# An adaLN block on one core: a fixed setup order, buffer clears on another queue, and a re-cut passage from attention to the experts

## The chip, the core and the metric

The kernel runs on one core of one Trainium2 chip. A core has five engines that run their own instruction streams in order: TensorE (PE, matrix products, with weight loads shown apart as PEld), VectorE (DVE), ScalarE (ACT), GpSimd (POOL) and SyncE (SP, which here only issues transfers). Engines wait for each other on semaphores. Transfers (DMAs) are issued by SP, ACT or POOL and carried by 16 DMA engines. The metric is the device time of one execution in microseconds (us); less is better.

## The reference, cut to what matters

Two batches of 2048 tokens of width 256 pass through one block: layer norm with a shift and scale made from `c`, attention in a window of 128 tokens (16 heads of 64), a gated sum onto `x`, a second norm, and a mixture of 8 experts with two choices per token and a capacity of 640 tokens per expert and choice.

```python
x = L0_attn_x
mod = (_silu(L0_c) @ L0_wmod).reshape(L0_c.shape[0], 6, 1, -1)
sa, ca, ga, sb, cb, gb = (mod[:, 0], mod[:, 1], mod[:, 2], mod[:, 3], mod[:, 4], mod[:, 5])
ga = (2 * (ga >= 0) - 1) * jnp.maximum(jnp.abs(ga), 0.25)      # gb likewise
h = _layernorm(x, axis=-1) * (1 + ca) + sa
x = x + ga * _L0_attn_ref(h, L0_attn_Wqkv, L0_attn_Wout)
h = _layernorm(x, axis=-1) * (1 + cb) + sb
x = x + gb * _L0_ffn_ref(h, L0_ffn_gate_w, ...)
...
for c in range(K):                       # in _L0_ffn_ref: two choices, 8 experts
    pos = jnp.take_along_axis(jnp.cumsum(oh, axis=0) - 1, idx[:, None], axis=1)[:, 0]
    keep = pos < CAP
    buf_idx = jnp.where(keep, idx * CAP + pos, n_slots)
    xbuf = jnp.zeros((n_slots, Dm), x.dtype).at[buf_idx].set(x, mode='drop')
    hmid = jax.nn.relu(jnp.einsum('ecd,edf->ecf', xb, W1) + b1[:, None, :])
    yb = jnp.einsum('ecf,efd->ecd', hmid, W2) + b2[:, None, :]
    y = y + ytok * (prb * keep.astype(prb.dtype))[:, None]
```

## The kernel before

**Products in three passes.** Operands of the large products are split into a rounded high part and a low remainder: ACT copies the high part (`nc.scalar.copy`), and DVE or POOL subtracts it from the raw value for the low part (`split`, line 124). `passes` (227) then multiplies high by high, high by low and low by high.

**Setup** (322 to 463). SP loads `c`, the first x group, wmod (two loads), six pieces of wqkv and two halves of wout; ACT's queue loads three small tensors. `load_split` (139) loads a piece into a `raw` buffer, of which the pools `stage` and `sp` have two each, and splits it; the low parts of wqkv pieces 1, 2 and 4 and of wout half 1 are made on POOL, the rest on DVE. From `c` come the modulation columns `cols` (PE, DVE) and the rows `wide4` (441 to 453), which go to memory as `rowd` and come back spread over all partitions (`rows`, `gbr`). A tile `blank` (461), which takes a `raw` buffer of `stage` too, holds an empty row. The order of this part is the planner's, which places each instruction by its own estimate of times.

**Attention** runs in a written-out order. From line 1156 on, `tc.manual_schedule` makes every engine, SP among them, follow the program's order. Tokens go in 16 groups of 256; each group has 8 pairs of heads; an iteration `w` (1084) takes two pairs, so there are NW = 64 iterations and three more to drain. It pipelines four stages: new pairs get scores (PE), then masking: `pack` (510) copies the own block on ACT (line 526) and lays the earlier block over it with DVE's masked copy (`copy_predicated`, 527), `maximum` (534) and ACT's `exps`; pairs one iteration older are normalized (POOL); pairs two older are transposed (`turn`), masked on POOL (`unpack`, 584 and 588) and multiplied by the values; pairs three older go through wout (`out_project`), for which a half of wout serves four head pairs of each group, the second half the last four. PE's results lie in a ring of six PSUM banks (`bank`).

**Side work** is put into places of an iteration by hand: `place(work, w, at)` (1039) says at which letter (A, B, M, H, C, S, V, in this order within an iteration) of which iteration the next step of a generator is traced. C stands just before the scores and `pack`, S just after `pack`, V at the end. So are placed the norm of the next group (`NORM`), the eleven steps of `close(g)` (633: gated sum, store, second norm, routing, counting, scatter of the rows to `xbuf` with POOL's indirect transfers; `CLOSE`, and `LATE` for the last groups), the weights of experts 0 and 1 (`Expert.steps`, 177: load, split), and the first item of expert work. At the start of iterations 1 to 4, `clear` (465) fills four pieces of `xbuf` each, 16 in all, from `blank`; ACT's queue issues them.

**Passage and experts.** Each expert's up to 10 tiles of 128 rows are cut into items (840 to 846): expert 0 in five of 2 tiles (q = 0 to 4), expert 1 in 4, 2, 2, 2 (q = 5 to 8), the others from 6 or 4. An item is loaded from `xbuf` (`load_slots`, 859), transposed and split (`turn_slots`, 877), and goes through `first_layer` and `second_layer` for 8 slices of the hidden width (`layers`, 1049). So that items 0 and 1 can begin before the last groups are routed, the last two groups' rows are kept out of the first EARLY = 4 tiles of expert 0: `totals` (737) counts what earlier groups brought and `shift` moves the late rows behind. In `close`, `totals` writes its product into the bank `cnt` ahead of the two products for `counts`, and DVE reads it as `both` (744). After the loop (1162 on) the last steps of `close(15)` alternate with item 1's layers, then item 5 runs, then item 2, the rest of expert 0 under run-time conditions (`further`, 1238), item 6, and so on.

Of the kernel before, what the change touches and what calls it, by code (L numbers as in the profile page):

```python
# [8 lines left out]
FP = mybir.dt.float32  # L9
FR = mybir.dt.float32r  # L10
I32 = mybir.dt.int32
# [17 lines left out]
def adaln_block_kernel(  # L29
# [41 lines left out]
    EARLY = 4 * P  # L71
# [62 lines left out]
    def load(src, shape, name, pool=stage):  # L134
        raw = pool.tile(shape, FP, tag="raw", name=f"raw_{name}", bufs=2)
        nc.sync.dma_start(out=raw, in_=src)
        return raw

    def load_split(hi, lo, src, shape, name, scale=None, pool=stage, eng=nc.vector):
        split(hi, lo, load(src, shape, name, pool), scale, eng)  # L140
# [99 lines left out]
    def norm(g):  # L240
# [13 lines left out]
        for k in range(ND):  # L254
            for t in range(SBT):
                nc.tensor.transpose(
                    tp[:, k * TS + t * P : k * TS + (t + 1) * P], z[:, t, k * P : (k + 1) * P], ident
                )
        hT = wk.tile([P, ND, TS], FP, tag="t2", name=f"hT_{g}")
# [61 lines left out]

    first = norm(0)
    with tc.tile_pool(name="setup", bufs=1) as sp:
# [5 lines left out]
        nc.sync.dma_start(out=wm[:, :, 0 : 2 * D], in_=wmv[:, :, 0 : 2 * D])  # L329
        gw = sp.tile([E, D], FP, name="gw")  # L330
        nc.scalar.dma_start(out=gw, in_=gate_w)
        b1r = sp.tile([E * NF, P], FP, name="b1r")
        nc.scalar.dma_start(out=b1r, in_=b1.rearrange("e (k p) -> (e k) p", p=P))
        nc.scalar.dma_start(
            out=gbias, in_=gate_b.rearrange("(a e) -> a e", a=1).to_broadcast([P, E])
        )
        make_identity(nc, ident)
# [30 lines left out]

        sg = sp.tile([B * ND, P], FP, name="sg")
# [3 lines left out]
        nc.vector.tensor_tensor(sg, sg, cr, ALU.mult)  # L373
        tp = bank("tp_c")
        nc.tensor.transpose(tp[:, 0 : B * ND], sg, ident[0 : B * ND, 0 : B * ND])
        scT = sp.tile([P, B, ND], FP, name="scT")
        nc.vector.tensor_copy(scT.rearrange("p b k -> p (b k)"), tp[:, 0 : B * ND])
        mc = bank("mod_cols")
        for m in range(2):
            for d in range(ND):  # L380
                o = (m * ND + d) * B
                for k in range(ND):
# [6 lines left out]
                    )  # L389
        colf = cols.rearrange("p m d b -> p (m d b)")  # L390
# [4 lines left out]

        for _ in first:
            pass

        for i in range(2):
            for j in range(3):  # L400
                f = slice(j * HD + i * HD // 2, j * HD + (i + 1) * HD // 2)
                load_split(
                    wq[:, 0, :, f], wq[:, 1, :, f], wqkv[:, f].rearrange("(k p) f -> p k f", p=P),
                    [P, ND, HD // 2], f"wq{i}_{j}", QSCALE if j == 0 else None,
                    pool=sp if (3 * i + j) % 2 else stage,
                    eng=nc.gpsimd if j == 1 or (i, j) == (0, 2) else nc.vector,
                )
        nc.sync.dma_start(out=wm[:, :, 2 * D :], in_=wmv[:, :, 2 * D :])
        for i in range(2):
            s = slice(i * NP // 2, (i + 1) * NP // 2)  # L410
            load_split(
                wo[:, 0, s, :], wo[:, 1, s, :],
                wout[i * HD // 2 : (i + 1) * HD // 2, :].rearrange("(k p) d -> p k d", p=P),
                [P, NP // 2, D], f"wo{i}", pool=stage if i else sp,
                eng=nc.gpsimd if i else nc.vector,
            )
        part(*project_qk(0, 0, 0))

# [8 lines left out]
        nc.vector.tensor_copy(b1T, tp[:, 0 : E * NF])  # L427

# [4 lines left out]
        for g in range(2):  # L433
# [16 lines left out]
            if g == 0:  # L450
                nc.vector.tensor_copy(wide4[:, 1, :], plain)
            else:
                nc.vector.tensor_scalar(wide4[:, 2, :], plain, 1.0, None, ALU.add)
        nc.sync.dma_start(out=rowd, in_=wide4)
# [3 lines left out]


        xs[1] = load_x(1)  # L460
        blank = stage.tile([P, ROW], FP, tag="raw", name="blank")
        nc.gpsimd.memset(blank, 0.0)
        nc.gpsimd.memset(blank[:, TOK : TOK + 1].bitcast(I32), 2 * T)

    def clear(i):

        for r0 in range(i * BUF, (i + 1) * BUF, CAP):
            nc.scalar.dma_start(
                out=xbuf[r0 : r0 + CAP, :].rearrange("(p n) d -> p n d", p=P),
                in_=blank.rearrange("p (a d) -> p a d", a=1).to_broadcast([P, CAP // P, ROW]),  # L470
            )

# [160 lines left out]
    def close(g):  # L633
# [103 lines left out]
        def totals(j, o):  # L737

            nc.tensor.matmul(
                out=cnt[:, o : o + KC * E], lhsT=ones,  # L740
                rhs=pref[:, j, :, :].rearrange("p k e -> p (k e)"), start=True, stop=True,
            )
            both = small.tile([P, KC, E], FP, tag="both", name=f"both_{g}_{o}", bufs=2)
            nc.vector.tensor_scalar(
                both.rearrange("p k e -> p (k e)"), cnt[:, o : o + KC * E], float(CAP), None, ALU.min
            )
            total = small.tile([P, E], FP, tag="total", name=f"total_{g}_{o}", bufs=2)
# [3 lines left out]
        if late:  # L751

            e = g - (NG - 2)
            total = totals(j0, n)
            nc.vector.tensor_scalar(
                shift[:, e : e + 1], total[:, e : e + 1], -1.0, float(EARLY), ALU.mult, ALU.add
            )
            nc.vector.tensor_scalar(shift[:, e : e + 1], shift[:, e : e + 1], 0.0, None, ALU.max)
# [7 lines left out]
        nc.vector.tensor_copy(counts, cnt[:, 0:n])  # L766
        yield
# [36 lines left out]
        if late:  # L804
            rows_of = NSLOT - EARLY
# [26 lines left out]
        if g == NG - 1:  # L832

            total = totals(NT, n)
# [8 lines left out]
    for e in range(E):  # L843
        head = 2 if e == 0 else 4 if e in (1, E - 1) else WIDE
        ends = [0, *range(head, NB + 1, 2)]
# [31 lines left out]
    def turn_slots(q, n0):  # L877

        tiles = items[q][1]
        if n0 == 0:  # L880
            w = len(tiles)
            if q and (w > 2 or items[q - 1][0] in (1, E - 1) and items[q - 1][1].start == 0):
                w = WIDE
            xTs[q] = [
# [412 lines left out]
```

## Time and profile before

| What | us |
|---|---|
| median of three runs (lowest, highest) | 1161.58 (1160.19, 1163.09) |
| the profiled execution | 1161.56 |
| its span, first to last instruction | 1159.8 |
| PE busy in the span | 1086.3 (94%) |
| weight loads busy | 999.6 (86%) |
| DVE busy | 877.4 (76%) |
| ACT busy | 676.7 (58%) |
| POOL busy | 593.8 (51%) |
| mean granted clock of PE | 0.970 |

The page gives busy time of each engine, the span in 40 slices with the PE clock that was granted (1.00 is full), groups of instructions by line with their mean duration and the idle time of the engine before them, and the transfers with the time from issue to landing. In a timeline, a line has the start, the duration, the engine (ACTq and SPq are the queues that issue transfers), the line of the kernel, the operation, output and inputs, and in brackets how long the engine stood before it and what released it. L127 is the subtraction or copy in `split`, L232 any product in `passes`.

### The profile page before, as it was taken

To read this page: it belongs to the slowest core of one execution; us is meant where nothing else is said; L and a number is where in the kernel's file an instruction comes from. 1 tells how busy PE (TensorE), PEld (TensorE's weight loads), DVE (VectorE), ACT (ScalarE), POOL (GpSimd) and SP (SyncE) were. 2 spreads that over 40 slices of the span, in tenths; PEclk is the share of its full clock that TensorE was granted. 3 is DMA by queue.
4 is the path that set the end of the run, shared out by engine and by line. 5 is a ranking of instruction groups with operands and counts; after the bars stand their busy time and mean duration, and the time that the engine had idled before them with its cause. 6 is when DMAs were issued, how large, how long until landed. Compare 5 with 4: busy or idle time off the path is not lost. (4 is left out here: it accounts for less than half of the span.)

```text
span 1159.8 us, 25187 instructions
## 1 busy us (share of the span) xinstructions
PE 1086.3 (94%) x9246; PEld 999.6 (86%) x9246; DVE 877.4 (76%) x2168; ACT 676.7 (58%) x2097; POOL 593.8 (51%) x769
## 2 busy tenths in 40 slices
PE   6799999999999999999999997779889999999995
PEld 4678999999999888999999896768879999999995
DVE  6556688888878778888878877767667777878764
ACT  4467776777777567777777676423344444344441
POOL 4235465665675556665675665433522615443524
PEclk9899999999999999999999998879989999999998
DMA  6890010010010010010010022233432524342413
GB/s 228 194 218 21 1 39 19 21 39 19 21 39 19 21 43 29 21 36 20 17 37 20 18 65 70 85 91 95 83 106 87 84 84 90 83 89 67 83 45 36
DMA packets 59571, 72.09 MB, mean 62 GB/s; under 512 B 4807, under 2 KB 51152, under 8 KB 59436
## 3 DMA queue, kind: packets, MB, share of 16 engines
q1 hardware_dynamic: 36988, 44.27, 12.2%
q0 software_dynamic: 11712, 14.79, 7.4%
q10 hardware_dynamic: 10736, 11.27, 4.3%
q8 instruction: 80, 1.31, 0.5%
q14 instruction: 55, 0.45, 0.1%
HBM read 40.11 MB, written 32.27 MB: 62 GB/s over the span
## 5 line engine op out<-in xcount | busy, mean ns | idle before, releaser
L937 ACT ACTIVATE hm<-ph,b1T 128x256 fp32r<-128x256 f32 (+2 forms) x184 | 99.3, 540 | 224.8 <-PE ph L232 192.6
L232 PE MATMUL pq<-hh,wq 128*128 128x256 f32 x1024 | 216.8, 295 | 3.5 <-ACT hh L268 3.0
L232 PE MATMUL ph<-xT,we 128*128 128x256 f32 (+2 forms) x1104 | 203.6, 325 | 15.5 <-DVE xT L127 4.6
L550 ACT ACTIVATE pm<-pm,mx 128x128 f32<-128x128 f32 x512 | 204.1, 402 | 19.4 <-DVE mx L536 16.7
L232 PE MATMUL y<-we,hm 128*128 128x256 f32 x1440 | 201.5, 285 | 6.6 <-DVE hm L939 6.6
L232 PEld LDWEIGHTS y<-we,hm 128*128 128x128 f32 x1440 | 186.7, 190 | 10.7 <-DVE hm L939 9.3
L232 PEld LDWEIGHTS ph<-xT,we 128*128 128x128 f32 x1104 | 172.3, 196 | 21.2 <-issue 6.5
L584 POOL TENSOR_SCALAR_AFFINE_SELECT pT<-pT 128x512 f32<-128x512 f32 (+1 forms) x128 | 80.9, 632 | 211.6 <-ACT pT L583 211.5
L232 PEld LDWEIGHTS pq<-hh,wq 128*128 128x128 f32 x1024 | 170.0, 193 | 5.8 <-ACT hh L268 3.4
L938 DVE TENSOR_SCALAR r<-ph,b1T 128x256 f32<-128x256 f32 (+2 forms) x184 | 101.8, 562 | 73.1 <-ACT hm L937 65.6
L560 POOL TENSOR_TENSOR pm<-pm,rd 128x512 f32<-128x512 f32 x128 | 133.8, 1045 | 28.5 <-DVE rd L558 26.4
L232 PE MATMUL pq<-hl,wq 128*128 128x256 f32 x512 | 145.8, 285 | 0.0
L526 ACT COPY pm<-sc 128x256 f32<-128x256 f32 (+1 forms) x256 | 80.6, 363 | 107.9 <-PE sc L502 70.3
L1002 POOL TENSOR_TENSOR ys<-ys,gw 128x256 f32<-128x256 f32 x56 | 48.4, 971 | 175.7 <-DVE ys L992 157.0
L607 PE MATMUL av<-pT,v 128*64 128x128 f32 (+1 forms) x1472 | 126.7, 321 | 4.7 <-POOL pT L588 2.2
L607 PEld LDWEIGHTS av<-pT,v 128*64 128x64 f32 x1472 | 91.1, 140 | 33.7 <-POOL pT L588 4.6
L1003 POOL DMA_INDIRECT out_dram<-ys,tok x60 | 98.1, 1634 | 33.5 <-issue 11.4
L527 DVE COPY_PREDICATED pm<-within,sc 128x256 f32<-128x256 int32 (+1 forms) x256 | 96.1, 422 | 22.0 <-ACT pm L526 21.1
L502 PE MATMUL sc<-kr,qh 64*128 64x256 f32 (+1 forms) x1024 | 105.7, 296 | 5.0 <-DVE ql L300 2.0
L550 ACT ACTIVATION_READ_ACCUMULATOR pm<-pm,mx 128x1 f32 x512 | 99.6, 194 | 0.0
L232 PEld LDWEIGHTS pq<-hl,wq 128*128 128x128 f32 x512 | 99.0, 193 | 0.0
L939 DVE TENSOR_TENSOR hm<-r,hm 128x256 fp32r<-128x256 f32 (+2 forms) x144 | 94.6, 657 | 5.3
(162 smaller groups left out, 2261.9 us busy)
## 6 DMA issues: line engine op xcount, KB each, us to landing
raw_w<-in_L_ffn_W_dram SPq DMA_DIRECT2D x32, 512.0 KB, 3.9
xbuf<-blank ACTq DMA_DIRECT2D x16, 685.0 KB, 9.6
xt<-xbuf SPq DMA_DIRECT2D x8, 822.0 KB, 4.9
x<-in_L_attn_x_dram SPq DMA_DIRECT2D x16, 256.0 KB, 2.8
out_dram<-x SPq DMA_DIRECT2D x16, 256.0 KB, 2.3
xt<-xbuf SPq DMA_DIRECT2D x7, 548.0 KB, 5.0
raw_wq<-in_L_attn_Wqkv_dram SPq DMA_DIRECT2D x6, 512.0 KB, 7.0
wm<-in_L_wmod_dram SPq DMA_DIRECT2D x1, 1024.0 KB, 11.1
```

What stands on the lines that cost most here:

```text
L232: nc.tensor.matmul(out=out_, lhsT=a, rhs=b, start=start and n == 0 and i == 0, stop=stop and n == last and i == 2, **kw,)
L502: nc.tensor.matmul(out=sc[h][:, t, lo:], lhsT=q[r, t * P : (t + 1) * P], rhs=kr[r, (0, 1, 0)[i], hp, blk, :], start=(i == 0), stop=(i == 2),)
L526: nc.scalar.copy(pm[:, h, ts, :], blocks[:, own, :])
L527: nc.vector.copy_predicated(pm[:, h, ts, :], within.rearrange("p (a k) -> p a k", a=1).to_broadcast([P, n, P]), blocks[:, before, :],)
L550: nc.scalar.activation(pm[:, h, t, :], pm[:, h, t, :], AF.Exp, bias=mx[:, h, t : t + 1], accum_out=den[:, h, t : t + 1],)
L560: nc.gpsimd.tensor_tensor(pmv, pmv, rd.rearrange("p h (t a) -> p (h t) a", a=1).to_broadcast([P, 2 * SBT, P]), ALU.mult,)
L584: nc.gpsimd.affine_select(out=pT[:, :, t0:, 0, :], in_=own[:, :, t0:, :], pattern=[[0, 2], [0, n], [-1, P]], compare_op=ALU.is_gt, fill=0. ...
L607: nc.tensor.matmul(out=av[h * DH : (h + 1) * DH, q0 : q0 + hi - lo], lhsT=v[:, f0 + h * DH : f0 + (h + 1) * DH], rhs=pT[:, h, lo:hi], star ...
L937: nc.scalar.activation(hh[:, s], phv, AF.Relu, bias=bias)
L938: nc.vector.tensor_scalar(r[:, s], phv, bias, 0.0, ALU.add, ALU.max)
L939: nc.vector.tensor_tensor(hl, r[:, 0:W], hh, ALU.subtract)
L1003: add = nc.gpsimd.indirect_dma_start(out=of, out_offset=bass.IndirectOffsetOnAxis(ap=tok[:, 0:1], axis=0), in_=y, in_offset=None, bounds_c ...
```

## The change

Setup: the order is fixed by hand from its first instruction on. The loads move to SP; the six wqkv pieces have five `raw` buffers of their own; their high parts (ACT) and low parts (now all on DVE) are written out one by one between the other steps; wout is no longer split there. `blank` is filled early. Then, ahead of the loop, SP issues wout's half 0, x group 2 and all 16 clears; a generator splits wout's half 0 at (1,A), where it also issues the load of half 1, and splits half 1 at (1,C).

```diff
-    def load(src, shape, name, pool=stage):
-        raw = pool.tile(shape, FP, tag="raw", name=f"raw_{name}", bufs=2)
+    def load(src, shape, name, pool=stage, bufs=2):
+        raw = pool.tile(shape, FP, tag="raw", name=f"raw_{name}", bufs=bufs)
...
+    order = tc.manual_schedule(engines=everything)
+    order.__enter__()
     first = norm(0)
...
+        for n in range(3):
+            get(n)
...
+        nc.sync.dma_start(out=wm[:, :, 2 * D :], in_=wmv[:, :, 2 * D :])
+        xs[1] = load_x(1)
+        for n in range(3, 5):
+            get(n)
...
+        blank = stage.tile([P, ROW], FP, tag="raw", name="blank", bufs=2)
...
+        high(0)
+        low(0)
...
+        high(1)
         for _ in first:
             pass
...
+        low(1)
+        high(2)
         part(*project_qk(0, 0, 0))
+        low(2)
+        high(3)
+        part(*project_qk(0, 0, 1))
+        get(5)
...
+        low(3)
+        high(4)
+        low(4)
+        high(5)
...
+        low(5)
         nc.sync.dma_start(out=rowd, in_=wide4)
         load_rows(0)
...
-    def clear(i):
-
-        for r0 in range(i * BUF, (i + 1) * BUF, CAP):
-            nc.scalar.dma_start(
+    def clear():
+
+        for r0 in range(0, NSLOT, CAP):
+            nc.sync.dma_start(
                 out=xbuf[r0 : r0 + CAP, :].rearrange("(p n) d -> p n d", p=P),
...
+    def load_output():
+
+        for i in range(2):
+            s = slice(i * NP // 2, (i + 1) * NP // 2)
+            raw = load(
+                wout[i * HD // 2 : (i + 1) * HD // 2, :].rearrange("(k p) d -> p k d", p=P),
+                [P, NP // 2, D], f"wo{i}",
+            )
+            yield
+            split(wo[:, 0, s, :], wo[:, 1, s, :], raw)
...
-        for i in range(2 * w - 2, 2 * w):
-            if 0 <= i < E:
-                clear(i)
...
+    outputs = load_output()
+    next(outputs)
+    xs[2] = load_x(2)
+    clear()
+    place(outputs, 1, ["0A", "0C"])
     for w in range(NW + 3):
         iteration(w)
```

Passage: `totals` gets a bank of its own and is traced after `counts`; EARLY becomes 4 tiles for expert 0 and 2 for expert 1; expert 1 is cut into 2, 4, 2, 2 tiles; the norm's step is split in two; places move; item 1 is loaded at (64,V) and turned before the pools of attention close.

```diff
-    EARLY = 4 * P
+    EARLY = (4 * P, 2 * P)
...
-        head = 2 if e == 0 else 4 if e in (1, E - 1) else WIDE
-        ends = [0, *range(head, NB + 1, 2)]
+        head = 2 if e < 2 else 4 if e == E - 1 else WIDE
+        ends = [0, 2, *range(6, NB + 1, 2)] if e == 1 else [0, *range(head, NB + 1, 2)]
...
-    NORM = ["0B", "1A", "1H", "2A", "2B"]
+    NORM = ["0B", "1A", "1H", "1H", "2A", "2B"]
...
-        NG - 3: ["0H", "1A", "1B", "2B", "2H", "3A", "3B", "3H", "3C", "3C", "3C"],
-        NG - 2: ["0H", "1A", "1B", "2B", "2H", "2C", "3A", "3B", "3M", "3C", "3C"],
+        NG - 3: ["0H", "1A", "1B", "2B", "2H", "3A", "3B", "3H", "3C", "3C", "4C"],
+        NG - 2: "0H 1B 1V 2H 2C 2V 3A 3B 3H 3C 3V".split(),
...
-    place(experts[0].pieces, NW - 4, "0A 2B 2C 3B 3C".split())
-    place(experts[1].pieces, NW - 1, "0B 1B 1C 2M 3A".split())
-    place(first, NW - 2, "0A 1H 1S 2B 2H 2V 3B 3H 3V 4A".split())
+    place(experts[0].pieces, NW - 4, "0A 2B 2S 3S 3V".split())
+    place(experts[1].pieces, NW, "0A 0V 1M 1V 2B".split())
+    place(first, NW - 2, "1A 1C 1V 2B 2H 2V 3B 3H 3V 4A".split())
...
+        if w == NW:
+            load_slots(1)
...
     next(last)
     next(first)
+    turn_slots(1, 0)
...
-    load_slots(1)
     load_slots(5)
     load_b2(1)
-    turn_slots(1, 0)
...
-        if f in (6, 8):
-            turn_slots(5, f - 6)
+        if f == 6:
+            turn_slots(5, 0)
     load_slots(2, 2)
-    load_slots(6, 2)
+    load_slots(6)
...
-        if f == 6:
+        if f == 7:
             turn_slots(2, 0)
...
+            2: [fills],
+            3: [do(turn_slots, 6, 0)],
+            5: [do(turn_slots, 6, 2)],
+            7: [do(turn_slots, 3, 0)],
...
+    more[0].append(do(load_slots, 7, 1))
```

## The prediction

> **What bounds the kernel now.** I read the span and times first (profiled execution 1161.56 us, of which the span is 1159.8 and 1.76 lies around it; median of the runs 1161.58, so sums made against the profile carry over unchanged), then the busy time by windows, then the timelines of ScalarE (ACT), SyncE's queue (SP) and VectorE (DVE) in the two stretches that the diff touches: the first 95 us and 690 to 870 us.
>
> Busy time by windows (us, then busy us and instructions of PE, weight loads, DVE, ACT, POOL, the granted clock, the DMA share, GB/s):
>
> ```profile
> 36.00:38.00 2.00, 0.54 (x3) 0.11 (x1) 1.12 (x3) 1.81 (x9) 0.00 (x0) 1.00 0.28 100
> 46.00:48.00 2.00, 2.00 (x12) 2.00 (x11) 1.61 (x5) 0.27 (x1) 0.00 (x0) 0.50 1.11 236
> 58.00:60.00 2.00, 2.00 (x15) 1.33 (x12) 1.48 (x5) 0.38 (x2) 0.00 (x0) 0.50 1.13 253
> ...
> 100.00:200.00 100.00, 100.00 (x966) 90.59 (x967) 76.94 (x212) 73.06 (x257) 57.94 (x80) 1.00 0.07 22
> ...
> 760.00:765.00 5.00, 0.19 (x2) 0.17 (x2) 3.71 (x10) 0.00 (x0) 2.45 (x6) 0.84 0.74 237
> 765.00:770.00 5.00, 3.34 (x13) 2.65 (x14) 1.76 (x4) 1.31 (x3) 0.72 (x1) 0.50 0.59 166
> ```
>
> From 100 to 690 us PE is full at full clock: no time can be gained or caught up there, and whatever shifts its start shifts the end. Before 95 us and between 705 and 860 us PE has gaps; those are what the change can move. In the first stretch the 16 clears of `xbuf` saturate the DMA engines (share 1.1 at about 235 GB/s) from 36 to 86 us.
>
> Timeline of ACT around the first clears, then tile `blank`, then tile `x` in the first 40 us and tile `raw_wo`:
>
> ```profile
> 36.21 0.56 ACTq L468 DMA_DIRECT2D xbuf<-blank  x1
> ...
> 38.91 1.49 ACTq L468 DMA_DIRECT2D xbuf<-blank  x1
> 40.44 0.40 ACT L550 ACTIVATE pm<-pm,mx 128x128 f32<-128x128 f32 x1 [2.46 <-DVE z L248]
> ```
>
> ```profile
> L468 ACTq DMA_DIRECT2D xbuf<-blank x16: 521/983/2000, 36.2 to 76.5; - x16
> ...
> DMA to landing us min/median/max: 5.2/9.6/11.6
> ```
>
> ```profile
> L205 SPq DMA_DIRECT2D x<-in_L_attn_x_dram x3: 416/862/892, 1.3 to 6.0; - x3
> ...
> DMA to landing us min/median/max: 2.9/11.2/11.3
> ```
>
> ```profile
> DMA to landing us min/median/max: 4.2/4.2/4.2
> ```
>
> To be seen: while ACT's sequencer issues four clears, ACT stands (2.46 us here; 2.50, 1.94 and 2.85 in the next three iterations). And on SP a 256 KB load of `x` that lands in 2.9 us at the head of the queue took 11.2 us when it was issued behind four wqkv pieces and `wm`: a load on SP lands after what was queued ahead of it.
>
> Waits between 690 and 870 us:
>
> ```profile
> POOL xbuf L819 <- DVE sslot L816: 14.9, 2, 10.4
> ...
> PE cnt L759 <- DVE both L744: 6.0, 2, 4.4
> ...
> PE tp_x L895 <- DMA xt<-xbuf: 5.5, 2, 4.8
> ...
> ACT pm L550 <- DVE mx L536: 5.0, 2, 4.2
> ```
>
> **The change, part by part.**
>
> *Setup in program order, low parts on DVE.* On POOL three wqkv low parts cost 4.68 for two and 2.38 for one, wo's 3.73; on DVE one costs 1.21 us alone, but 3.08 while POOL ran its own, and the tiny `sgn` (0.41) became 2.26 and 2.49. After: six low parts on DVE, 7.3 us, with nothing of POOL beside them. I walked the new DVE order with these durations: `low(0)` ends at 11.4 (as now), hT and hl to 14.4, `low(1)` 15.6, ql 18.3, `low(2)` 19.5, kr 20.3, gwT and b1T 20.7, `low(3)` and `low(4)` 23.1, the two gates' rows 2 x 2.05 to 27.2, `low(5)` 28.4, then two q/k low parts and the norm statistics of group 1, 2.4, so iteration 0's masking starts near 31 instead of 32.66: a gain of about 2 us (bounds 0 and 3).
>
> *Clears from ACT to SP.* ACT's four holes go: 9.75 us of ACT, nearly all on the path, as PE is then fed by ACT (it idles in the same iterations): -2.5 us before iteration 1's masking, -7.3 us in iterations 2 to 4.
>
> *What is queued behind the clears.* SP now runs in program order: `wide4` ready 27.2, so rowd 27.3, rows and gbr about 28.7 to 30 (1.4 us after rowd, as now), wo half 0, x_2, all 16 clears from about 31, and only then wo half 1, whose load is traced at (1,A). Its split is at (1,C): an ACT copy, in order, ahead of iteration 1's masked copies. ACT would get there at about 38 (42.94 is the copy ahead of it now, less 1.8, 2.46 and some clock). The clears are 11.22 MB at 235 GB/s: 47.7 us. Ahead of them on the queue lie rows, gbr, wo half 0 and x_2 (1.4 MB, some 6 us from 28.7), so their data runs from about 35 to 84 and wo half 1 lands near 86. ACT stands for 48 us; behind it are the masked copies, DVE's low part and maxima, then PE: it has 6 banks, four of which hold the scores, and stops two banks into iteration 2. Lower bound: the clears' data starts at 31 and nothing delays the rest, 80. Upper: the load must take `blank`'s buffer (the pool has two), so it is issued only when the last clear has landed, plus 4.2: 90.
>
> Here two passages of the Trainium skill's "DMA: Bandwidth & Descriptors" pull apart. "Issuing engines are not separate DMA queues" says all engines' DMAs interleave on the same 16 DMA engines and that another issuer saves only issue time: by that alone the move is worth the 9.75 us and costs nothing, and wo half 1 takes its share early. "Queues, rings and completion order" has descriptors of one queue consumed in ring order. The 11.2 us row is of the second kind, and I take it.
>
> From the wait on: iteration 1's masking starts near 87.5 (44.9 now). From there to iteration 5's masking takes 47.95 us now (92.85). After, less 7.3 for ACT's holes, and plus a restart in half clock. For that the skill's "TensorE: Matmul & The Clock Gate" ("What's actually happening") gives about 3.4 us of work until full clock, 1.7 us lost; this trace, after a gap of 3 us at 36.5, stayed at 0.50 from 40 to 49.3, 4.6 lost. Part of it hides behind ACT, so 2, less some 1 for half clocks of now in 46 to 60. So 41.5, iteration 5 masks at 129 instead of 92.85: **+36 us** (bounds +30 and +40). PE is full afterwards; nothing gives it back.
>
> *Passage, splits behind the masked copies.* At (62,C) and (63,C) a split (1.2 to 2.1 us on DVE) ran ahead of `copy_predicated`; ACT waited 5.0 us in two waits for the maxima, PE 2.2, 0.9, 0.7 and 2.8 us. Now they are at S and V, and the closing steps of group 14 and first_layer move likewise. About 6 us of PE gaps; the same DVE work returns in iterations 64 and 65, which are PE's lightest: -5 (bounds 0 and -8).
>
> *Totals apart.* The 4.4 us at `both` isn't the bank alone: the next product also needs `oh` and `pref`, done at 745.3, 0.4 us before PE starts. For group 14 it frees 0.4, for group 15 also little: -0.5. Two more instructions: none; one more bank name in the ring of six, later two.
>
> *Item 1 loaded and turned early; item 5 of 2 tiles.* PE's idle 760 to 764.8 (the xt landing), 1.5 more for the split and half clock to 778 (about 5) go. But group 15's chain (norm, route, count, scatter) has to end before item 2 can be loaded. Now it runs from 758.7 to the last scatter at 795.3, and the 4-tile item 5 covers it and the load; item 2 begins at 814, or 802.5 if two tiles (11.5 us of PE) are taken off, as they are done later. After: f=0 at 762, tp_f at 764.6 (h is done at 764.5 as now), pl 766, counts 774, sslot 783, scatters (4 x 1.3) 788, landed 790, load 4.7 us, turn and split: item 2 at 796.5, PE idle for some 5 us before it. Gain 6 (bounds +2 if the shorter item 5 leaves more of the load bare, and -11).
>
> *Item 6 of 4 tiles.* It carries expert 2's four splits and three turns, and PE lost 3.6 us in it between 835 and 850; twice the products cover them better: -2 (bounds +2, -4). Late step orders, `load_slots(7)` in item 6, fills one step earlier: 0, hidden by full PE; +1 without it.
>
> Passage together: **-13** (bounds -20 and 0). Sum: +36 - 13 = +23, 1161.6 + 23 = **1184**.
>
> **Rivals.**
> - *The forecast*, 0.75: the wait for wo half 1 and most of the passage gain. Its own range is 1170 to 1198.
> - *wo half 1 lands early* (the queue serves it beside the clears), 0.15: then -2 - 9.75 - 13, about 1137: faster. For it: the first rule above, and that four clears land 5 to 12 us after issue. Against it: those same landings rise one by one, as in a line, and the `x` row. It decides by the landing time: the setup's loss is 13, equal to the passage's gain, when wo half 1 lands near 63 us; earlier is faster, later is slower.
> - *The passage gains nothing*, 0.10: group 15's chain stays as long as now and the 2-tile item 5 bares 5 to 10 us of the load ahead of item 2. Then +36 and 0 to +3: about 1199. For it: scatters waited 14.9 us for slot numbers, a chain of small DVE steps that the change leaves. Against it: 10 us of idle and half clock at 760 to 778 that have nothing to do with that chain.
>
> **How the numbers follow.** Slower by over 0.3% (about what a measurement of this kernel can tell from no change): nearly all of the first and third, 0.84. Faster: the second, 0.14. Within: 0.02, only where the landing falls near 63. The range 1168 to 1200 holds the first and nearly all of the third; the second is left out.
>
> **What would show it.** Right: ACT's cast of `wo` half 1 waits over 40 us for `raw_wo`, PE nearly empty from 42 to 86, the masking of iteration 5 near 129; no ACT holes at clears; no `tp_x` wait at item 1 but one of some 5 us at item 2. Wrong: `raw_wo` lands before 63, or the clears run faster on SP than 235 GB/s, or PE catches up before 100.

## The result, and the profile after

The changed kernel takes 1192.86 us (median of 4 runs, 1192.70 to 1195.61) against 1162.34 us (4 runs, 1160.19 to 1163.36): ratio 1.0268, 95% interval 1.0249 to 1.0288. It is slower by 30.5 us. The profiled execution took 1192.72 us, its span 1191.0 us at a mean granted clock of 0.958 (before: 1161.56, 1159.8, 0.970).

Busy time by windows of the changed kernel; the columns are the window's ends and length, then busy us and instructions of PE, PEld, DVE, ACT, POOL, then the granted clock, the DMA share and GB/s:

```profile
46.00:48.00 2.00, 0.00 (x0) 0.00 (x0) 0.00 (x0) 0.00 (x0) 0.00 (x0) 0.76 1.11 233
58.00:60.00 2.00, 0.00 (x0) 0.00 (x0) 0.00 (x0) 0.00 (x0) 0.00 (x0) 0.50 1.11 247
80.00:85.00 5.00, 0.00 (x0) 0.00 (x0) 0.00 (x0) 0.00 (x0) 0.00 (x0) 0.50 0.96 214
100.00:200.00 100.00, 99.87 (x933) 89.94 (x930) 72.04 (x189) 75.41 (x272) 52.28 (x75) 1.00 0.04 12
755.00:760.00 5.00, 0.00 (x0) 0.00 (x0) 0.18 (x1) 0.44 (x3) 4.79 (x8) 0.50 0.60 196
760.00:765.00 5.00, 4.32 (x38) 3.74 (x40) 1.81 (x4) 1.81 (x6) 0.12 (x1) 0.62 0.03 8
```

Two things are to be seen. From 45 to 86 us all five engines stand, while the DMA engines carry what they carried before. And PE stands once more, from 755 to 760.7, for item 0's rows, for which it did not wait before. What the first is shows in the timelines of SP's queue and of ACT and in the waits from 20 to 140 us:

```profile
29.85 0.43 SPq L136 DMA_DIRECT2D raw_wo<-in_L_attn_Wout_dram  x1
...
30.93 41.66 SPq L500 DMA_DIRECT2D xbuf<-blank  x16
72.69 2.76 SPq L136 DMA_DIRECT2D raw_wo<-in_L_attn_Wout_dram  x1
```

```profile
39.26 0.58 ACT L316 COPY v<-pv 128x512 f32<-128x512 f32 x1
86.65 1.04 ACT L127 CAST wo<-raw_wo 128x1024 fp32r<-128x1024 f32 x1 [46.80 <-DMA raw_wo<-in_L_attn_Wout_dram]
89.18 0.27 ACT L569 COPY pm<-sc 128x128 f32<-128x128 f32 x1 [1.49 <-DVE pm L562]
...
128.73 1.36 ACT L569 COPY pm<-sc 128x256 f32<-128x256 f32 x4 [1.52 <-PE sc L545]
```

```profile
ACT wo L127 <- DMA raw_wo<-in_L_attn_Wout_dram: 46.8, 1, 46.8
...
PE tp L617 <- DVE pm L570: 45.4, 1, 45.4
```

SP issues the 16 clears of 685 KB in one run of 41.66 us. The first two take 0.6 us each; from the fifth on an issue takes 3.05 us in the mean (12 of them from 36.13 to 72.69), and the clears land 3.0 us apart (from 43.3 to 85.3): SP can issue no faster than they are carried. Only then does it come to wo half 1. Its transfer lands 13.9 us after its issue (tile `raw_wo`, longest). ACT came to the cast at 39.8 and stood until 86.65. Behind the cast, in ACT's order, is the masking of iteration 1. Iteration 5 is masked from 128.73 on; in the kernel before it was

```profile
92.85 1.36 ACT L526 COPY pm<-sc 128x256 f32<-128x256 f32 x4 [1.52 <-PE sc L502]
```

**Where the time is, in two parts.** PE's last group of value products in iteration 62, the first one that waits for POOL's `pT` after 690 us, is a good marker: ahead of it PE is full, behind it comes the passage. Before, and then in the changed kernel with item 0's rows:

```profile
712.65 1.97 PE L607 MATMUL av<-pT,v 128*64 128x256 f32 x12 [2.20 <-POOL pT L588]
```

```profile
747.30 1.09 PE L650 MATMUL av<-pT,v 128*64 128x256 f32 x12 [1.12 <-POOL pT L631]
...
760.68 1.09 PE L940 MATMUL tp_x<-ident,xt 128*128 128x128 f32 x4 [5.80 <-DMA xt<-xbuf]
```

So the front part became 34.65 us longer, and the part from the marker to the end of the span 3.45 us shorter (447.15 to 443.70). Five profiled kernels with this change's passage put the second part at 443.1 to 443.8, two with the old passage at 447.2 and 447.6: it repeats within 0.7 us, better than the medians do, and I use it below for the passage. The front part of kernels with one and the same setup spreads over 3 us (700.9 to 703.6). Two things limit the marker. The wait in its own brackets, 1.12 us here and 2.20 before, lies ahead of it but belongs to the passage: counted with it, the passage is 4.6 us shorter and the front part 35.7 longer. And one profile is one execution: of how long PE runs at half clock behind the marker it shows only one case.

### The profile page after: what moved, and what is told of

It is laid out like the page before. It is cut to its first block, busy times and chain, and to the rows that moved or that the text cites. A ratio compares the mean times of both kernels' runs of the same rounds, so it can differ in the third digit from the quotient of the medians.

```text
span 1191.0 us, 25196 instructions
## 1 busy us (share of the span) xinstructions
PE 1077.3 (90%) x9246; PEld 994.5 (83%) x9246; DVE 875.2 (73%) x2172; ACT 675.8 (57%) x2097; POOL 581.5 (49%) x765
## 5 line engine op out<-in xcount | busy, mean ns | idle before, releaser
L229 PE MATMUL ph<-xT,we 128*128 128x256 f32 (+2 forms) x1104 | 198.5, 320 | 9.7 <-PEq L1285 3.7
L229 PEld LDWEIGHTS ph<-xT,we 128*128 128x128 f32 x1104 | 168.2, 192 | 14.9 <-issue 4.2
L650 PE MATMUL av<-pT,v 128*64 128x128 f32 (+1 forms) x1472 | 124.2, 317 | 3.8 <-POOL pT L631 1.1
L617 PE MATMUL tp<-ident,pm 128*128 128x128 f32 x512 | 80.6, 282 | 47.8 <-DVE pm L570 47.8
L617 PEld LDWEIGHTS tp<-ident,pm 128*128 128x128 f32 x512 | 56.8, 141 | 59.1 <-issue 48.7
```

What stands on the lines that cost most here:

```text
L229: nc.tensor.matmul(out=out_, lhsT=a, rhs=b, start=start and n == 0 and i == 0, stop=stop and n == last and i == 2, **kw,)
L617: nc.tensor.transpose(tp[:, h, t, :], pm[:, h, t, :], ident)
L650: nc.tensor.matmul(out=av[h * DH : (h + 1) * DH, q0 : q0 + hi - lo], lhsT=v[:, f0 + h * DH : f0 + (h + 1) * DH], rhs=pT[:, h, lo:hi], star ...
```

## Experiments

**Theory**: in the front part, wo half 1 is held on SP behind the clears, and ACT, in order, stands for it. In the passage, the change gives less than forecast because it also made item 0's rows late. **Rivals**: the clears' traffic itself slows the start, or another setup edit does; the passage is set by group 15's or group 14's chains of small steps, whatever is moved.

The twelve experiments and both kernels, with the first of ACT's copies that begin the masking of iteration 5 ("it. 5"), the marker and the rest of the span behind it, from each one's profile (p1 to p7 leave the front part alone):

| kernel | median us | ratio to before, 95% interval | it. 5 | marker | rest |
|---|---|---|---|---|---|
| before | 1161.4 to 1163.0 | | 92.85 | 712.65 | 447.15 |
| the change | 1192.86 | 1.0268 (1.0249 to 1.0288) | 128.73 | 747.30 | 443.70 |
| e1 split of half 1 late | 1160.00 | 0.9988 (0.9975 to 1.0002) | 92.54 | 711.28 | 443.82 |
| e2 both halves first | 1146.58 | 0.9871 (0.9849 to 0.9893) | 81.88 | 700.87 | 443.83 |
| e3 half 1 on ACT's queue | 1181.21 | 1.0183 (1.0145 to 1.0221) | 117.24 | 735.99 | 443.61 |
| e4 clears back on ACT | 1162.20 | 1.0007 (0.9996 to 1.0017) | 100.08 | 718.86 | 443.14 |
| b1 before, clears on SP | 1150.26 | 0.9905 (0.9887 to 0.9922) | 81.52 | 701.57 | 447.63 |
| p1 e2, group 13 earlier | 1142.38 | 0.9850 (0.9822 to 0.9878) | | 701.36 | 439.04 |
| p2 p1, item 0 at 62 V | 1143.47 | 0.9855 (0.9830 to 0.9881) | | 703.34 | 438.56 |
| p3 e2, splits at C | 1144.33 | 0.9848 (0.9830 to 0.9867) | | 701.14 | 443.06 |
| p4 e2, items as before | 1153.22 | 0.9931 (0.9911 to 0.9951) | | 701.33 | 449.87 |
| p5 p1, item 0 at 62 C | 1143.07 | 0.9848 (0.9831 to 0.9864) | | 703.39 | 436.51 |
| p6 p5, splits at C | 1139.38 | 0.9812 (0.9795 to 0.9828) | | 702.32 | 436.38 |
| p7 p6, item 1 late | 1144.62 | 0.9855 (0.9824 to 0.9886) | | 703.61 | 437.29 |

### The front part

**e1**, the wait moved, the queue left:

```diff
-    place(outputs, 1, ["0A", "0C"])
+    place(outputs, 1, ["0A", "4B"])
```

> Only the place of the split of wo half 1 moves, from iteration 1 to iteration 5, just ahead of its first use; its load stays behind the 16 clears on SP. Theory (ScalarE, in order, stood 46.8 us before that cast): the load still lands near 86 us, but ScalarE now reaches the cast near 74 us and waits some 12 us, so iteration 5 is masked near 93 us instead of 128.7 and the time is about 1157 us (1150 to 1162). Rival (the stretch is slow because the clears fill the DMA engines, or because of the other setup edits, and the wait is only where that shows): iteration 5 stays above 120 us and the time above 1180 us.

Its timeline of ACT has the same cast:

```profile
84.44 1.04 ACT L127 CAST wo<-raw_wo 128x1024 fp32r<-128x1024 f32 x1 [7.36 <-DMA raw_wo<-in_L_attn_Wout_dram]
```

The load landed nearly as late as in the change (84.4), and the clears ran as they did; only ACT came to the cast at 77.1 instead of 39.8 and stood 7.4 us. Iteration 5 came 36.2 us earlier. The rival is out.

**e2**, the queue changed, the splits left where they are:

```diff
-        for i in range(2):
-            s = slice(i * NP // 2, (i + 1) * NP // 2)
-            raw = load(
+        halves = [
+            load(
                 wout[i * HD // 2 : (i + 1) * HD // 2, :].rearrange("(k p) d -> p k d", p=P),
                 [P, NP // 2, D], f"wo{i}",
             )
+            for i in range(2)
+        ]
+        for i in range(2):
+            s = slice(i * NP // 2, (i + 1) * NP // 2)
             yield
-            split(wo[:, 0, s, :], wo[:, 1, s, :], raw)
+            split(wo[:, 0, s, :], wo[:, 1, s, :], halves[i])
...
-        blank = stage.tile([P, ROW], FP, tag="raw", name="blank", bufs=2)
+        blank = cl.tile([P, ROW], FP, tag="h2T", name="blank", bufs=1)
```

> Both halves of wo are loaded ahead of the clears on SP, the blank tile sits in a buffer of its own, and the splits stay where the change has them. Theory (order in SP's queue): half 1 lands near 38 to 42 us, ScalarE hardly waits, iteration 5 is masked near 81 to 84 us (that of the kernel before, 92.85, less 2.3 and less the 9.75 of ScalarE's holes) and the time is about 1146 us (1143 to 1152), faster than before. Rival (the clears' traffic itself is what delays): the 16 clears still run 47 us at 235 GB/s beside iterations 1 to 4, iteration 5 stays above 110 us and the time above 1170 us.

It gave what the theory said to 0.6 us. Windows of e2, to be held against those of the change above:

```profile
46.00:48.00 2.00, 2.00 (x15) 1.91 (x15) 0.96 (x3) 2.00 (x10) 0.15 (x1) 0.96 1.11 247
58.00:60.00 2.00, 2.00 (x13) 1.74 (x12) 0.74 (x2) 2.00 (x9) 1.55 (x3) 1.00 1.10 243
```

The DMA engines are as full as before, at the same GB/s, and PE is full too. Iterations 1 to 4 last 9.99, 10.02, 9.36 and 10.21 us here, beside the clears (each from its first ACT copy to the next one's), and 9.98, 10.01, 9.35 and 10.21 in the change, where the clears are over by then: their traffic costs nothing that can be seen. What hurts is standing behind it.

**e3**, the same load from another queue, the clears left on SP:

```diff
-            raw = load(
-                wout[i * HD // 2 : (i + 1) * HD // 2, :].rearrange("(k p) d -> p k d", p=P),
-                [P, NP // 2, D], f"wo{i}",
-            )
+            raw = stage.tile([P, NP // 2, D], FP, tag="raw", name=f"raw_wo{i}", bufs=2)
+            (nc.scalar if i else nc.sync).dma_start(
+                out=raw,
+                in_=wout[i * HD // 2 : (i + 1) * HD // 2, :].rearrange("(k p) d -> p k d", p=P),
+            )
```

> Half 1 of wo is loaded by a DMA that ScalarE issues at the same place of the program, the clears stay on SP. Theory (what counts is the queue of the issuer): issued near 39 us it overtakes the clears' descriptors and lands between 43 and 55 us in spite of full DMA engines; iteration 5 is masked at 82 to 95 us and the time is 1146 to 1159 us. Rival (the 16 DMA engines serve everything in the order of issue, whatever engine issued it): it lands near 75 to 86 us, iteration 5 near 120 to 129 us, time 1184 to 1193 us.

Both were wrong on the time. Timeline of ACT:

```profile
64.23 0.41 ACTq L510 DMA_DIRECT2D raw_wo<-in_L_attn_Wout_dram  x1
64.69 0.40 ACT L594 ACTIVATE pm<-pm,mx 128x128 f32<-128x128 f32 x1 [27.70 <-DMA xbuf<-blank]
75.17 1.05 ACT L127 CAST wo<-raw_wo 128x1024 fp32r<-128x1024 f32 x1 [7.40 <-DMA raw_wo<-in_L_attn_Wout_dram]
```

ACT stood 27.7 us before it could issue the load at all, and what released it was a clear. The landing records of the trace show why that can be: in this program the transfers of SP and ACT take eight landing counters (semaphores) in turn, and the counter that this load got had last been used by a clear that landed at 64.16 us; ACT's wait for that counter ended at 64.18. Once issued, the load landed in 10.9 us, at 75.1, while the clears (16.1 us in the median) went on until 84 us: on its own queue it did pass a clear that SP had issued 1 us ahead of it and that landed at 80.2. So the queue matters, as the theory said, but the wait for the counter came first and I had not thought of it. What ACT would do with a free counter wasn't tried.

**e4**, the clears back on ACT, all else as changed:

```diff
-    def clear():
+    def clear(i):
-        for r0 in range(0, NSLOT, CAP):
-            nc.sync.dma_start(
+        for r0 in range(i * BUF, (i + 1) * BUF, CAP):
+            nc.scalar.dma_start(
...
+        for i in range(2 * w - 2, 2 * w):
+            if 0 <= i < E:
+                clear(i)
...
-    clear()
```

> The clears go back to ScalarE, four in each of iterations 1 to 4 as before; all else is the changed kernel. Theory: half 1 of wo lands near 38 us, ScalarE's four holes (9.75 us) are back, iteration 5 is masked near 90.5 us (92.85 less the 2.3 that the new setup order gave), and the time is about 1155 us (1152 to 1159), the passage's gain of some 4.7 us and 2.3 us better than before. Rival (another setup edit holds iteration 1, not the clears): iteration 5 above 115 us, time above 1175 us.

The rival fell (100, not 115), but my number was 7 us too low. ACT's timeline and SP's waits:

```profile
48.83 1.04 ACT L127 CAST wo<-raw_wo 128x1024 fp32r<-128x1024 f32 x1 [7.45 <-DMA raw_wo<-in_L_attn_Wout_dram]
```

```profile
SPq L136 <- DVE wo L127: 4.7, 1, 4.7
```

Even with an empty queue half 1 comes late: with `blank` and half 0 in the two `raw` buffers, its load waits for half 0's split, and SP issues it only at 39.69. With the clears on SP this second wait lies hidden in the first. Beside that, ACT's holes are back: 100.08 less 81.88 of e2 is 18.2, of which 7.45 is this wait; the other 10.75 I put down to the holes and what they do to PE (b1, next, has 11.33 for them).

**b1**, the kernel before with one edit, in `clear`:

```diff
-            nc.scalar.dma_start(
+            nc.sync.dma_start(
```

> The kernel before the change with one edit: the 16 clears are issued by SP instead of ScalarE, at the same four places. wo is loaded in the setup there, so nothing is queued behind them. Theory (the clears' price is ScalarE's 9.75 us of holes, and full DMA engines cost TensorE nothing): iteration 5 is masked near 83 us instead of 92.85 and the time is 1152 us (1150 to 1155). Rival (the holes are not on the path, or SP's queue holds something that is needed): 1158 us or more.

Iteration 5 comes 11.33 us earlier, the time falls by 11.3: ACT's 9.75 us of holes and 1.6 us more. Its SP queue holds things up as well, but nothing that is needed soon:

```profile
42.27 18.88 SPq L468 DMA_DIRECT2D xbuf<-blank  x7
61.20 3.02 SPq L119 DMA_DIRECT2D rows<-rowd  x1
```

`rows` is loaded at 61 instead of 31.9; its first reader, the closing of group 0, comes only at 90.33. e2, with all setup edits, has iteration 5 at 81.88, b1, with none of them, at 81.52: the new setup order is worth 2.3 us at iteration 0 (30.67 for 32.98 in the change), and the two splits of wo in iteration 1, which were in the setup before, take it back: from iteration 0 to 1 it takes 9.36 us in b1 without a split, 10.73 in e1 with one and 11.85 in e2 with two.

### The passage

The base is e2, whose passage is the change's. **p1** moves one step back:

```diff
-        NG - 3: ["0H", "1A", "1B", "2B", "2H", "3A", "3B", "3H", "3C", "3C", "4C"],
+        NG - 3: ["0H", "1A", "1B", "2B", "2H", "3A", "3B", "3H", "3C", "3C", "3C"],
```

> The kernel with both halves of wo ahead of the clears (1146.6 us), with one step moved back in the passage: the last closing step of group 13, which scatters its rows, is at C of iteration 61 as before the change, not at C of iteration 62. Theory (the change moved this scatter one iteration later and with it the load of item 0, for which TensorE stood 6.41 us): the load is issued near 707 us instead of 711.3, TensorE's wait at item 0 falls from 6.4 to 1 to 2 us and some half clock behind it goes; 1141 us (1138 to 1143). Rival (group 14's chain of small VectorE and GpSimd steps sets this stretch): the gap comes back at the transposes of group 14 or at its counts, 1145 to 1148 us.

The rest of the span is 4.8 us shorter, so the theory holds and group 14's chain moved along with the rest (its transposes wait 2.5 us as in e2). Of the 4.8 us, 1.1 is given back ahead of the marker, where PE waits 2.20 us for `pT` again: with the scatter in iteration 61 POOL comes to `pT` straight from it, 2.5 us ahead of PE's stop; in e2 it had stood for 8.2 us and began 3.6 us ahead. So the late scatter cost 3.7 us. But TensorE's wait at item 0 is still 3.27, more than expected. SP's timeline and its waits from 680 to 730 us in p1:

```profile
701.88 0.38 SPq L695 DMA_DIRECT2D out_dram<-x  x1
705.08 0.37 SPq L136 DMA_DIRECT2D raw_w<-in_L_ffn_W_dram  x1
705.50 0.50 SPq L904 DMA_DIRECT2D b<-in_L_ffn_b_dram  x1
706.09 0.39 SPq L917 DMA_DIRECT2D xt<-xbuf  x1
```

```profile
SPq L136 <- DVE al L298: 14.1, 2, 11.1
```

Item 0's load (`xt`) is right behind a load of expert 0's weights, and that one waits for the buffer that the split at S of iteration 62 frees; before the change the split stood at C. (DVE's record just ahead of `al` is that split, at 703.84.) **p2** puts item 0's load at V of iteration 62, which is still behind it:

```diff
-    place(first, NW - 2, "1A 1C 1V 2B 2H 2V 3B 3H 3V 4A".split())
+    place(first, NW - 2, "0V 1C 1V 2B 2H 2V 3B 3H 3V 4A".split())
```

> As the kernel with group 13's scatter one iteration earlier, and item 0's load issued at the end of iteration 62 instead of in iteration 63. Theory (item 0's load): no wait for it is left; 1 to 2 us less than with the scatter alone, 1139 us (1136 to 1142). Rival (group 14's chain): no more than 0.5 us from the scatter alone.

The rest of the span is 0.5 us shorter, which is the rival's number; but the load is issued 4.73 us behind the marker in p1 and in p2, and PE still waits 3.0 us for it, so this edit did not bring the load forward. **p5** puts it at C of iteration 62, ahead of the split (the same line with `0C` for `0V`):

> As the kernel with both halves of wo ahead of the clears and group 13's scatter one iteration earlier (1142.4 us), with item 0's load issued at C of iteration 62, ahead of the split that now stands behind the masked copies. Theory (on SP the load of the next piece of expert 0's weights waits for that split, and item 0's load was queued behind it): item 0's load is issued near 702 us instead of 706.1, nothing of TensorE's 3.3 us wait at item 0 is left, 1139 us (1136 to 1141). Rival (group 14's chain is next in line): the wait moves to the transposes of group 14 (2.5 us now, then 5), 1141.5 to 1143.5 us.

The load is issued 1.45 us behind the marker. PE's waits at the two places, from 675 to 860 us:

```profile
PE tp_f L720 <- POOL h L708: 2.7, 1, 2.7
PE tp_x L943 <- DMA xt<-xbuf: 2.6, 1, 2.6
```

The one wait left for `xt` is at item 2 (787.63); item 0 has none, group 14's transposes (`tp_f`) wait 2.7 us and not the rival's 5, and the rest of the span is 2.5 us shorter than p1's, nearly what the wait was. By the profile the theory holds. The time does not show it: 1143.07 us lies in the rival's range and 0.7 above p1's (their intervals overlap, and p5's marker came 2 us later).

**p3** puts the splits back ahead of the masked copies, on e2, **p6** does the same on p5:

```diff
-    place(experts[0].pieces, NW - 4, "0A 2B 2S 3S 3V".split())
+    place(experts[0].pieces, NW - 4, "0A 2B 2C 3B 3C".split())
```

> The kernel with both halves of wo ahead of the clears (1146.6 us), with the splits of expert 0's weights back ahead of the masked copies (at C of iterations 62 and 63). The prediction's sum gave this part of the change 5 us: 1151.6 us (1149 to 1154). Rival (the splits only change places with other VectorE work, and VectorE's waits move): within 1.5 us of 1146.6.

> As the kernel with item 0's load ahead of the split, and the splits of expert 0's weights ahead of the masked copies as before the change. The prediction's 5 us for the splits' new place: 1144 us. Theory (that place gains nothing, as the masked copies' waits only change places with later ones): within 1.5 us of the kernel with item 0's load ahead, or 1 to 3 us below it, since the closing of group 14 starts earlier.

The rest of the span changes by -0.8 (p3) and -0.1 (p6), the medians by -2.3 and -3.7: the splits' new place gains nothing and may cost some us. PE's waits from 675 to 860 us, first of e2, then of p3:

```profile
PE tp_x L943 <- DMA xt<-xbuf: 9.3, 2, 6.4
...
PE tp_f L720 <- POOL h L707: 2.4, 1, 2.4
...
PE po L229 <- DVE al L298: 1.9, 1, 1.9
...
PE tp L620 <- DVE pm L573: 1.2, 1, 1.2
```

```profile
PE tp_x L943 <- DMA xt<-xbuf: 7.3, 2, 4.1
...
PE tp L620 <- DVE pm L573: 2.3, 1, 2.3
...
PE po L229 <- DVE al L298: 0.7, 1, 0.7
...
PE tp_f L720 <- POOL h L707: 0.5, 1, 0.5
```

With the splits behind, `tp` waits 1.1 us less for the masked copies, but `po` waits 1.2 more for `al`, which now stands behind the split on DVE, and group 14's transposes (`tp_f`) and item 0's rows (`tp_x`) are waited for 1.9 and 2.3 us longer. That is 4.3 us of waits, and only 0.8 of it is in the span: other waits take 1.2 back, and behind the marker PE is busy 2.4 us longer in p3 (395.7 for 393.3) with the same 2902 instructions, at a mean clock of 0.94 for 0.95. In the medians p6 is 3.7 us below p5; of that 1.1 lies ahead of the marker and 0.1 behind it, so most of it isn't in the profiled pair, and what it is stays open (p6's profiled execution is the slowest of its four, p5's the fastest).

**p4** cuts the items as before (item 5 of 4 tiles, item 6 of 2, with the loads and turns that go with them), on e2; item 1 stays early. EARLY goes with it, as group 15's rows are kept out of the first tiles of expert 1, those of item 5, too: item 2 is the first that waits for them.

```diff
-    EARLY = (4 * P, 2 * P)
+    EARLY = (4 * P, 4 * P)
...
-        head = 2 if e < 2 else 4 if e == E - 1 else WIDE
-        ends = [0, 2, *range(6, NB + 1, 2)] if e == 1 else [0, *range(head, NB + 1, 2)]
+        head = 2 if e == 0 else 4 if e in (1, E - 1) else WIDE
+        ends = [0, *range(head, NB + 1, 2)]
```

> The kernel with both halves of wo ahead of the clears (1146.6 us), with the items cut as before the change (item 5 of 4 tiles, item 6 of 2); item 1 stays loaded and turned early. By the prediction's sum: TensorE's wait of 2.9 us at item 2 goes as 11.5 us more work covers group 15's chain, but the short item 6 loses some 3.6 us beside expert 2's splits; 1147 us (1144 to 1150). Rival (the cut is what made the passage shorter): 1151 us or more.

The rest is 6.0 us longer, so the rival is right: the new cut is the part of the passage that pays. The wait at item 2 goes, as forecast, but the loss behind it, where the short item 6 and its neighbours run, is larger than the 3.6 us counted: from 140 to 170 us behind the marker PE is busy 26.37 us at a clock of 0.89 in p4, 30.00 at 1.00 in e2. **p7** loads and turns item 1 after the attention part, as before, on p6:

```diff
-        if w == NW:
-            load_slots(1)
...
-    turn_slots(1, 0)
...
+    load_slots(1)
     load_slots(5)
     load_b2(1)
+    turn_slots(1, 0)
```

> The fastest kernel so far (both halves of wo ahead of the clears, group 13's scatter one iteration earlier, item 0's load ahead, splits back ahead of the masked copies: 1139.4 us), with item 1 loaded and turned after the attention part as before the change. By what the other runs leave over (the change's passage 4.5 us shorter; of that the item cut 6.6 shorter, the splits 2 to 4 longer, group 13's late scatter 4.2 longer) loading and turning item 1 early is worth 4 to 6 us: 1144.5 us (1143 to 1146), with a wait of TensorE for item 1's rows of 4 to 5 us. Rival (it only moves the wait to group 15's chain, and the 5 us come from elsewhere): within 1.5 us of 1139.4.

The median is where the theory put it, but its interval is wide (0.9824 to 0.9886), and the profile's rest of the span says 0.9 us, the rival's answer. PE's timeline in p7, and in p6 at the same two places:

```profile
755.66 1.11 PE L943 MATMUL tp_x<-ident,xt 128*128 128x128 f32 x4 [6.60 <-DMA xt<-xbuf]
...
790.76 0.66 PE L943 MATMUL tp_x<-ident,xt 128*128 128x128 f32 x4 [2.65 <-DMA xt<-xbuf]
```

```profile
750.97 1.43 PE L229 MATMUL ph<-xT,we 128*128 128x256 f32 x5 [2.41 <-DVE xT L127]
...
786.62 0.66 PE L943 MATMUL tp_x<-ident,xt 128*128 128x128 f32 x4 [2.04 <-DMA xt<-xbuf]
```

Item 1's rows are waited for 6.6 us instead of 2.4 for its split. At item 2 the two kernels are 2.85 us apart, counted from each one's marker (87.15 and 84.30), and at the end of the span 0.9. Where the waits went shows in the windows from the marker to the end, p6 and then p7:

```profile
702.32:1138.70 436.38, 394.73 (x2902) 381.00 (x2902) 324.54 (x617) 179.15 (x362) 182.04 (x211) 0.95 0.37 84
```

```profile
703.61:1140.90 437.29, 389.07 (x2902) 375.78 (x2902) 326.61 (x617) 179.52 (x362) 181.95 (x211) 0.96 0.37 84
```

PE stands 6.6 us longer in p7 (48.22 for 41.65) and is busy 5.7 us less for the same 2902 instructions, at a mean clock of 0.96 for 0.95. The five kernels with the change's passage lie between 392.1 and 394.5. And the profiles are of p7's fastest execution (clock 0.981, its others 0.974 to 0.978) and of p6's slowest (0.977, its others 0.980 and 0.981), so the 0.9 us leans on that pair. Item 1's early turn is worth 0.9 us by this pair and 5.2 by the medians; the waits speak for the upper part, and how much of the clock's difference the edit itself makes stays open.

p6, 1139.38 us, is the fastest of all: 0.9812 of before (0.9795 to 0.9828), 53 us below the change.

## Why the prediction was right, point by point

The forecast was 1184 us with 1168 to 1200; it was 1192.86, on the side and within the range, and for the reason given: ACT stood for wo half 1 behind the clears. The front part was forecast within 1.4 us. The error of 9 us is one term, the passage.

- **PE full, so what the start loses the end loses.** At iteration 5 and at the marker the differences against before were +35.9 and +34.7 in the change, +24.4 and +23.3 in e3, -11.0 and -11.8 in e2: within 1.4 us, both ways. Most of that is the shorter wait at the marker: from iteration 5 to the beginning of this wait 13 of the 14 kernels take 617.4 to 617.9 us, p7 618.6.
- **Setup order, -2.** Measured -2.3 at iteration 0; lost again by iteration 5 (b1 against e2), as the splits of wo moved into iteration 1 (e1). The prediction had no term for that; it was hidden under the wait.
- **ACT's holes, -9.75.** b1 gave -11.3: right, and a little small.
- **wo half 1 behind the clears.** Landing near 86, iteration 1 masked near 87.5, iteration 5 at +36: measured 86.65 (start of the cast), 89.18, +35.9. That the last agrees to 0.1 us is luck: iteration 1 came 1.7 us later than forecast, and the stretch from there to iteration 5 took 2.0 less (the term on the restart, below). Of the two passages of the Trainium skill's "DMA: Bandwidth & Descriptors", "Queues, rings and completion order" was the one that bore: the load was held in its queue. But of the wait 33 us (39.8 to 72.69) passed before the load was issued at all, since SP could not issue the clears faster than they were carried; the prediction had the load wait in the queue, not for its issue. "Issuing engines are not separate DMA queues" gives the issue time as what another issuer saves and as usually small beside the transfer; here 16 issues in a row took 41.66 us of SP, and in the kernel before, in fours, they made 9.75 us of holes on ACT. The prediction's upper bound, that the load takes `blank`'s buffer, did not come true: it took half 0's (e4).
- **Restart, +2 less 1.** From iteration 1 to iteration 5 the change took 39.55 us, e2 and b1, where PE had never stood so long, 39.58 and 39.56. The restart did cost clock: PE ran at 0.50 from 89.9 to 94.8, 4.9 us, longer than the 3.4 us of work that the skill's "TensorE: Matmul & The Clock Gate" ("What's actually happening") gives; but e2 and b1 run some 4 us at the start of this stretch at 0.50 as well (to 46.2 and 46.4). The half clock of the kernel before that I read as ending at 49.3 lasted to 50.0. The term should have been 0, and ACT's holes of iterations 2 to 4 -8.4 (47.95 to 39.56 in b1) instead of -7.3.
- **Passage, -13: the mis-sized term.** It measured -3.45 behind the marker, -4.6 with the wait ahead of it, and this is how it divides:
  - *Splits behind the masked copies*, -5 forecast, +0.1 to +0.8 measured (p3, p6; +2.3 and +3.7 in the medians). Of the four PE waits that I counted (2.2, 0.9, 0.7 and 2.8 us) only the 0.9 is for a masked copy; 2.2 is POOL's `pT` at the marker, and 0.7 and 2.8 are item 0's own split. And I counted waits that go and not those that come: `al` behind the split on DVE, the closing of group 14, and on SP the weights' load that waits for the split and item 0's load behind it.
  - *Item 1 early and items recut*, -8 forecast; the cut alone -6.0 (p4), item 1's early turn -0.9 in the profile (p7, on another base; -5.2 in the medians): -6.9, nearly right, or -11 with the median. Of the 5 us wait forecast at item 2, 2.95 came.
  - *"Late step orders ... 0, hidden by full PE; +1 without it"*: wrong. The last step of group 13 is a scatter. One iteration later it made item 0's rows late, and PE, which is not full there (the prediction's own reading has gaps from 705 us on), stood 5.80 us: +4.8, or +3.7 with the wait at the marker (p1). Item 0's load, moved from A of iteration 62 to A of 63, was late once more on SP: +2.5 in the profile (p5). Together +7.3.
  - *Totals apart*, -0.5 forecast: not tried by itself. The product for `counts` waits 3.6 us for `oh` instead of 4.4 for `both`, so `oh` was the wait behind it, as argued.
  - These sum to +0.5 to +1.2 (7.3 - 6.9 + 0.1 to 0.8), on bases that differ, where -3.45 was measured: some 4 us of gain are not assigned by the profiles. The medians of the same five edits sum to -4.7 (splits by p6) or -6.1 (by p3), each edit uncertain by 3 to 4 us, and leave no gain over. So item 1's early turn is the likeliest place for the 4 us (its median says 5.2, its profile 0.9); the steps that were not moved one by one (totals, group 14's order, item 7's load) are not ruled out. That stays open.
- **Rivals.** "wo half 1 lands early" is out: it landed at 86.6, and e2 shows what an early landing gives (1146.58 us). "The passage gains nothing" was nearer than the forecast (its 1199 missed by 6, the forecast's 1184 by 9), but not for its reason: the wait ahead of item 2 was 2.95 us, not 5 to 10, and what took the gain was item 0.

## What to carry to other kernels

When a transfer moves to another queue, list what is issued behind it there and when each is needed: against SP with the loads in front (e2), the same 16 clears cost 11 us more on ACT (b1 against before) and 47 us more on SP with one load behind (iteration 5 at 128.73 for 81.88). A step that "only moves by one iteration" is to be followed to whatever reads its result from memory, through the queue that loads it: item 0's load was late once by a scatter, and once by a load ahead of it that waited for a split. Where the medians spread by 3 us, a marker in the trace that separates two stages tells more, if two things are looked at beside it: the wait at the marker itself, and how long PE was busy behind it with the same instructions, since that moved by 5.7 us between p6 and p7.

## What the runs showed of the hardware that was not expected

- SP's issue of a 685 KB transfer takes 0.6 us for the first two of a run and 3.05 us from the fifth on, the pace at which they land (the change: 16 in 41.66 us), and for that time nothing else of that queue is issued.
- DMA engines at a share of 1.10 to 1.12 and about 240 GB/s slowed nothing that can be seen: iterations 1 to 4 took 39.58 us beside the clears (e2) and 39.55 behind them (the change).
- A load from ACT's queue waited 27.7 us for a clear on SP's queue with which it shares no data (e3); by the landing records it waited for the landing counter, of which this program gives SP and ACT eight in turn.
